# Expert rows carry their share and their token number, and are added into the tokens' rows in memory by scattering DMAs, instead of being gathered back at the end

## The chip, the cores and the metric

The kernel runs on one core of one Trainium2 chip. The metric is device microseconds of that core for one execution of the whole program. Before the change the median of three runs is 2100.1 us (2098.34 to 2104.96). Engines are called PE (matrix engine), DVE (vector), ACT (scalar), POOL (GpSimd) and SP (sync, which here only issues DMAs).

## The reference

Two layers over x of 8 x 512 tokens with 256 features. Layer 0 is a bidirectional state-space block plus a top-1 mixture of experts; it is not touched by the change. Layer 1, cut to what matters:

```python
xn = layernorm(x)
x  = x + L1_attn(xn) + L1_ffn(xn)

# L1_attn: 16 heads of 16; scores * decay(|i - j|), clipped, softmax, values, output projection
# L1_ffn, over all 4096 tokens, 8 "experts" of which the last does nothing, top 2, capacity 512:
weights = softmax(x_flat @ router_w + router_b)
topk    = the two largest weights of a token, the rest 0
noop_w  = topk[:, -1]                       # the expert that passes the token through
sorted_indices = argsort(-mask, axis=0)[:cap]        # first 512 tokens of each real expert
inputs  = x_flat[used_idx] * sorted_mask             # (512, 7, 256)
h       = relu(inputs @ experts_inter)               # 256 -> 1024
out     = (h @ experts_out) * in_w                   # 1024 -> 256, times the token's weight
combined = zeros.at[used_idx].add(out)
combined = combined + x_flat * (noop_w * noop_mask)
```

## The kernel before

The change lies in the layer 1 part, which the profile shows from about 1105 us to the end. That part is one attention loop with other work slipped in.

**The attention loop.** `steps` (end of `tile_kernel`) lists 128 steps: 8 batches, 4 groups of 4 heads, 4 tiles of 128 query rows. In step n the program writes, for that n: `scores` of n (four products s_ps at L1379, four clips on DVE at L1384, four decay-and-max operations on DVE at L1386, and the negated maximum ng at L1390, once a step), the exponentials of step n-1 on ACT (L1394), the transposes of step n-2 (PE p_ps L1401, ACT copies pT L1402), and every second step the products with the values (o_ps L1410). ng is thus a clock of the loop: one at each step. When the four tiles of a group are done, `divide` sends the sums through memory: ACT copies them to os (L1420), SP stores od (L1421), one step later SP loads oT and sm back (L1431, L1432), one more step later DVE inverts sm (L1437), SP stores rd and loads rb (L1438, L1440), and two steps later DVE multiplies oT (L1443). After a batch's last group `finish` makes the output projection (PE fin L1323, ACT fo L1325, DVE x_sb L1327).

**Order.** The order on each engine is written out by hand: the whole loop stands in a manual schedule, and each engine runs its instructions in the order in which the Python code made them. Between the parts of a step, `fill` draws a piece of other work (first `urgent`: projections of the next batch and `finish`; then `idle`: the experts), and `more` draws from `rows` (the generator `combine`) when there is nothing else. SP, too, is one queue in program order: a DMA that waits holds all later ones.

**The experts.** First `late` ends layer 0, then `route1` finds two slots for each token, and `send_rows` scatters each token's row of xn1 into xd1 by 64 indirect DMAs on POOL (L1296) and begins the token's result x_sb (L1303) from the token's row x1, loaded at L1311, plus its pass-through part. `experts` then runs each of the 7 experts in two halves of 256 rows: load rows (L1209), transpose, two matrix layers (L1236, L1249), copy the result to e_yo (ACT L1254) and store it in yd1 (SP L1256).

**The end.** When the experts are through, `combine` takes the 32 token tiles one after the other, one for each call of `more`. For each it copies two slot numbers (DVE at L1316, in `turn`), issues two gathers from yd1 (POOL yg L1344), and for the tile six places earlier adds the two gathered rows, weighted with wsel, into x_sb (DVE L1358). With each batch's fourth tile `send` stores the batch in four DMAs of 128 KB (SP L1335), if `finish` has had its turn; otherwise `finish` sends it.

```python
held.append((i, [e2.tile([P, DM], FP, name="yg1", tag="row1", bufs=14) for _ in range(2)]))
...
if len(held) > 6:
    add(*held.pop(0))
```

Both e_xd and e_yo are drawn from one tag of two buffers, e_rows. x1, xd1 and yd1 are tensors in memory.

Of the kernel before, what the change touches and what calls it, by code (L numbers as in the profile page):

```python
# [37 lines left out]
NSLOT1 = NE1 * CAP  # L38
HALF = CAP // 2


# [16 lines left out]
def tile_kernel(ctx: ExitStack, tc: tile.TileContext, t, out: bass.AP):  # L58
# [35 lines left out]
    G.iota(iota_t, pattern=[[P, NTILE]], base=0, channel_multiplier=0, allow_small_or_imprecise_dtypes=True)  # L94
    iota_b = ctile("iota_b", [P, NBLK])
    G.iota(iota_b, pattern=[[1, NBLK]], base=0, channel_multiplier=0, allow_small_or_imprecise_dtypes=True)
    zero = ctile("zero", [P, DM])
    G.memset(zero, 0.0)
# [3 lines left out]
    yd0 = dram.tile([NBLK * P, DM], FP, name="yd0", tag="yd0")  # L102
    xd1 = dram.tile([NSLOT1, DM], FP, name="xd1", tag="xd1")
    yd1 = dram.tile([NSLOT1 + 1, DM], FP, name="yd1", tag="yd1")

    x1 = dram.tile([NT, DM], FP, name="x1", tag="x1")
    xtd = dram.tile([B, P, KC, S], FP, name="xtd", tag="xtd")
# [10 lines left out]
    def clear(dst, rows, lo, hi):  # L118

        n = rows // P  # L120
        A.dma_start(
            out=dst[: n * P, :].rearrange("(p r) d -> p r d", p=P)[:, lo:hi, :], in_=bc(zero, 1, [P, hi - lo, DM])
        )
# [275 lines left out]
    def route0():  # L399
# [29 lines left out]

        B3 = [P, NBLK, NE - 1]  # L430
        past = big.tile(B3, FP, name="past", tag="past")
        V.tensor_tensor(past, bc(end[:, : NE - 1], 1, B3), bc(iota_b, 2, B3), ALU.is_le)
# [48 lines left out]
    steps()  # L481
    l1c = tl = w_r = rb = w_q = w_o = w_uk = w_uv = w_kv = band = slot1 = wsel = proj1 = vt0 = qk0 = r1b = noop = None
    tls = ExitStack()
# [3 lines left out]
    with ExitStack() as es:  # L487
# [169 lines left out]
        def second_weights():  # L657

            nonlocal l1c, tl, w_r, rb, w_q, w_o, w_uk, w_uv, w_kv, band, slot1, wsel, proj1, vt0, qk0
            es.close()  # L660
# [13 lines left out]
            slot1 = ctile("slot1", [P, NTILE, 2], I32, l1c)  # L674
            wsel = [l1c.tile([P, NTILE], FP, name=f"wsel{k}", tag=f"wsel{k}") for k in range(2)]
            proj1 = ctile("proj1", [P, NTILE, NE], pool=l1c)
# [358 lines left out]
        with tc.manual_schedule(engines=ENGINES):  # L1035
# [39 lines left out]
            for n in range(N):  # L1075
# [43 lines left out]
                if n % 8 == 3 and n // 8 < NE1:  # L1119
                    e = n // 8  # L1120
                    clear(xd1, NSLOT1, TPB * e, TPB * (e + 1))
                    if e == 0:
                        A.dma_start(out=yd1[NSLOT1 : NSLOT1 + 1, :], in_=zero[0:1, :])
            last = batch[B - 1]
# [19 lines left out]
    with tc.tile_pool(name="a1", bufs=1) as p1, tc.tile_pool(name="a2", bufs=2) as p2, tc.tile_pool(  # L1144
# [9 lines left out]
        def route1():  # L1154
# [30 lines left out]

            V.tensor_tensor(noop, pr[:, :, NE1], mask[:, :, NE1], ALU.mult)


# [28 lines left out]
        def experts():  # L1217
            w1, xd = expert_w1(0), expert_rows(0, 0)
            yield
            for e in range(NE1):  # L1220
                w2 = e1.tile([P, FC, DM], FP, name="e_w2", tag="e_w2")
                Y.dma_start(out=w2, in_=t["eo"][e])
                for half in range(2):
                    at = slice(e * CAP + half * HALF, e * CAP + (half + 1) * HALF)
                    xdT = e1.tile([P, KC, HALF], FP, name="e_xdT", tag="e_xdT")
                    tp = bank("e_tp", [P, KC, HALF])
                    for k in range(KC):
                        for c in range(2):
                            T.transpose(tp[:, k, c * P : (c + 1) * P], xd[:, c, k * P : (k + 1) * P], ident)
                    A.copy(xdT, tp)  # L1230
                    yield
                    hT = e1.tile([P, FC, HALF], FP, name="e_hT", tag="e_hT")
# [10 lines left out]
                    elif e + 1 < NE1:  # L1243
                        w1, xd = expert_w1(e + 1), expert_rows(e + 1, 0)
                    yo = e2.tile([P, 2, DM], FP, name="e_yo", tag="e_rows")
# [87 lines left out]
        def send(b):  # L1333
            for i in range(b * TPB, (b + 1) * TPB):
                Y.dma_start(out=out[i * P : (i + 1) * P, :], in_=x_sb[:, i, :])  # L1335

        def combine():

            held = []
            for i in range(NTILE):  # L1340
                held.append((i, [e2.tile([P, DM], FP, name="yg1", tag="row1", bufs=14) for _ in range(2)]))
                at = turn(e2, i)
                for k in range(2):
                    G.indirect_dma_start(  # L1344
                        out=held[-1][1][k], out_offset=None, in_=yd1,
                        in_offset=bass.IndirectOffsetOnAxis(ap=at[:, k : k + 1], axis=0),
                        bounds_check=NSLOT1, oob_is_err=False,
                    )
                yield
                if len(held) > 6:  # L1350
                    add(*held.pop(0))
            for one in held:
                add(*one)

        def add(i, yg):
            xi = x_sb[:, i, :]
            for k in range(2):
                V.scalar_tensor_tensor(xi, yg[k], wsel[k][:, i : i + 1], xi, ALU.mult, ALU.add)  # L1358
# [290 lines left out]
```

## Time and profile before

| what | value |
|---|---|
| runs of the kernel | median 2100.1 us, 2098.34 to 2104.96, three runs |
| the profiled execution | 2129.08 us; span 2127.2 us; mean granted PE clock 0.929 |
| busy over the span | PE 88%, DVE 69%, ACT 55%, POOL 30% |
| layer 1 part | 1105 to 2127.2 us |
| scatters of `send_rows` | 64 on POOL, 1190.8 to 1318.2 us |
| experts | PE e_tp first at 1333.2, last e_yo at 1965.8 us |
| gathers of `combine` | 64 on POOL, 1969.6 to 2091.3 us |
| weighted additions of `combine` | 64 on DVE, 1994.6 to 2099.0 us, mean 479 ns |
| DMA, whole span | 263.67 MB; HBM read 193.44 MB, written 72.75 MB |

All times within the execution are microseconds from the start of the profiled span. "x4" is a number of instructions merged into a row, and the bracket at a row's end tells how long its engine was idle before and what ended that. A row of a stretch gives for each engine the busy time and the number of instructions that began in it, then the granted clock of PE (1.00 is full speed), the share of time that the 16 DMA engines were busy, and GB/s.

### The profile page before, as it was taken

The numbers are of one execution on the slowest core, as the hardware profiler recorded it, in microseconds if no ns is written. First come the engines' busy times: TensorE is split into PE (matmuls) and PEld (weight loads), VectorE is DVE, ScalarE is ACT, GpSimd is POOL, SyncE is SP. The second block draws the span as 40 slices with busy tenths as digits, with TensorE's granted clock in tenths as the row PEclk, the third lists the DMA queues.
The fourth block names the chain that finished last, engine by engine and source line by source line (L and its number), as shares of the span: only waits on it lengthen the run. The fifth ranks groups of instructions, "written<-read, shape, count | busy, mean of one in ns | idle before, by whom it ended". The sixth has DMA issues, their size and how long they took to land. (4 is left out here: it accounts for less than half of the span.)

```text
span 2127.2 us, 33330 instructions
## 1 busy us (share of the span) xinstructions
PE 1861.6 (88%) x11672; PEld 1231.4 (58%) x11672; DVE 1461.2 (69%) x3329; ACT 1179.0 (55%) x2545; POOL 643.6 (30%) x592
## 2 busy tenths in 40 slices
PE   5666999999999999986758788999999999999785
PEld 5333776767677677644535444656666666666443
DVE  5684757575575757687648886666666676767795
ACT  2243544445354544545327566777677777777663
POOL 0048645456464646345400353000000000000552
PEclk9877999999999999997858778999999999999787
DMA  7113745556555556435433342121221212221355
GB/s 259 58 55 128 239 154 190 182 170 208 169 199 181 179 172 193 126 110 158 142 96 110 104 136 76 65 96 61 66 80 62 97 59 87 65 74 56 95 108 95
DMA packets 156632, 263.67 MB, mean 124 GB/s; under 512 B 24906, under 2 KB 113022, under 8 KB 144562
## 3 DMA queue, kind: packets, MB, share of 16 engines
q1 hardware_dynamic: 124816, 144.70, 21.6%
q0 software_dynamic: 22320, 107.55, 16.4%
q10 hardware_dynamic: 9330, 9.31, 1.3%
q8 instruction: 92, 1.51, 0.3%
q14 instruction: 74, 0.61, 0.1%
HBM read 193.44 MB, written 72.75 MB: 125 GB/s over the span
## 5 line engine op out<-in xcount | busy, mean ns | idle before, releaser
L1384 DVE TENSOR_SCALAR s<-s_ps 128x512 f32<-128x512 f32 x512 | 317.8, 683 | 241.6 <-PE s_ps L1379 195.9
L1394 ACT ACTIVATE s<-s,ng 128x512 f32<-128x512 f32 x512 | 354.4, 727 | 32.8 <-DVE ng L1390 23.1
L1401 PE MATMUL p_ps<-ident,s 128*128 128x128 f32 x2048 | 301.5, 292 | 72.4 <-ACT pT L1402 61.6
L1401 PEld LDWEIGHTS p_ps<-ident,s 128*128 128x128 f32 x2048 | 247.6, 149 | 159.7 <-ACT pT L1402 91.4
L1402 ACT COPY pT<-p_ps 128x512 f32<-128x512 f32 x512 | 279.1, 590 | 91.0 <-PE p_ps L1401 63.3
L1386 DVE CUSTOM_DVE_ANT_0 s<-s,band 128x512 f32<-128x512 f32 x512 | 322.8, 688 | 0.0
L1344 POOL DMA_INDIRECT yg<-yd,at x64 | 68.3, 1067 | 705.1 <-ACT s L1394 650.4
L728 PE MATMUL pj<-xT,w_in 128*128 128x512 f32 x384 | 204.5, 660 | 16.0 <-DVE cv L741 14.2
L1379 PE MATMUL s_ps<-kT,qT 16*128 16x512 f32 x1024 | 174.1, 694 | 17.9 <-DVE s L1384 11.5
L541 PEld LDWEIGHTS h_ps<-xdT,w 128*128 128x128 f32 x1248 | 150.1, 193 | 21.0 <-issue 20.2
L541 PE MATMUL h_ps<-xdT,w 128*128 128x128 f32 x1248 | 153.7, 277 | 1.6 <-DMA w<-in_w_dram,w_idx 1.6
L741 DVE SCALAR_TENSOR_TENSOR cv<-pj,w_conv_w,cv 128x511 f32<-128x511 f32 (+2 forms) x192 | 143.1, 746 | 9.6 <-ACT cv L737 5.6
L559 PE MATMUL y_ps<-w,hT 128*128 128x256 f32 x624 | 147.4, 380 | 0.0
L904 POOL TENSOR_TENSOR au<-da,half 128x512 f32<-128x512 f32 x64 | 77.7, 1214 | 212.0 <-PE seg L920 108.1
L1410 PE MATMUL o_ps<-pT,vt 128*32 128x256 f32 x2048 | 139.0, 414 | 0.0
L559 PEld LDWEIGHTS y_ps<-w,hT 128*128 128x128 f32 x624 | 116.0, 191 | 32.1 <-issue 17.9
L728 PEld LDWEIGHTS pj<-xT,w_in 128*128 128x128 f32 x384 | 71.8, 205 | 100.3 <-issue 92.2
L978 POOL TENSOR_TENSOR yT<-yT,ex 128x512 f32<-128x512 f32 (+1 forms) x48 | 59.7, 1243 | 226.3 <-DVE ex L977 168.1
L1236 PE MATMUL e_hp<-e_xdT,e_w 128*128 128x256 f32 x448 | 121.7, 394 | 3.0 <-ACT e_xdT L1230 2.1
L1249 PE MATMUL e_yp<-e_w,e_hT 128*128 128x256 f32 x448 | 120.0, 390 | 0.2
L933 ACT ACTIVATE mt<-seg,mid 64x64 f32<-64x64 f32 x512 | 109.9, 310 | 0.8
L1410 PEld LDWEIGHTS o_ps<-pT,vt 128*32 128x32 f32 x2048 | 64.7, 117 | 77.5 <-issue 48.0
(275 smaller groups left out, 3028.8 us busy)
## 6 DMA issues: line engine op xcount, KB each, us to landing
ex<-exd SPq DMA_DIRECT2D x96, 128.0 KB
u<-in_u_dram SPq DMA_DIRECT2D x16, 512.0 KB
xtd<-xT SPq DMA_DIRECT2D x16, 512.0 KB
fr<-fdd SPq DMA_DIRECT2D x64, 128.0 KB
od<-os SPq DMA_DIRECT2D x32, 256.0 KB
xT<-xtd SPq DMA_DIRECT2D x15, 512.0 KB
e_w<-in_ei_dram SPq DMA_DIRECT2D x7, 1024.0 KB
e_w<-in_eo_dram SPq DMA_DIRECT2D x7, 1024.0 KB
```

Of the source, the lines that this page charges most:

```text
L541: T.matmul(hp[:, i, :], w1[:, k * FF + f * P : k * FF + (f + 1) * P], xdT[:, k * P : (k + 1) * P], start=(k == 0), stop=(k == KC - 1),)
L559: T.matmul(yp, hT[f // 4][:, f % 4, :], w2[:, f * DM : (f + 1) * DM], start=(f == 0), stop=(f == FC - 1))
L728: T.matmul(pj, w_in[:, k, o * P : (o + 1) * P], self.xT[:, k, :], start=(k == 0), stop=(k == KC - 1))
L741: V.scalar_tensor_tensor(cv[:, s:], pj[:, : S - s], conv_w[:, q, 3 - s : 4 - s], cv[:, s:], ALU.mult, ALU.add)
L1236: T.matmul(hp, w1[:, k, f * P : (f + 1) * P], xdT[:, k, :], start=(k == 0), stop=(k == KC - 1))
L1379: T.matmul(sp[i], self.q[r, cols], self.k[r, :], start=True, stop=True)
L1384: V.tensor_scalar(self.p[i], sp[i], -CLAMP, CLAMP, ALU.max, ALU.min)
L1386: V.tensor_tensor_reduce(out=self.p[i], in0=self.p[i], in1=band[:, at : at + S], scale=1.0, scalar=-3.0e38, op0=ALU.mult, op1=ALU.max, acc ...
L1394: A.activation(self.p[i], self.p[i], AF.Exp, bias=self.ng[:, i : i + 1])
L1401: T.transpose(pp[:, k, :], self.p[i][:, k * P : (k + 1) * P], ident)
L1402: A.copy(pT[i][:, :, cc * P : (cc + 1) * P], pp)
L1410: T.matmul(op[32 * i : 32 * i + 32, half * 2 * P : (half + 1) * 2 * P], self.v[:, k, h * (AD + 1) : h * (AD + 1) + 32], pT[i][:, k, :], st ...
```

## The change

A row sent to an expert gets 16 more columns: the 8 routing shares of its token and the token's number less 4096 (repeated 8 times). The experts' result is multiplied by the share as it leaves PSUM and is added by an indirect DMA straight into the token's row of x1 in memory; a row of an expert that holds no token (number 0, as cleared) goes to one of 128 spare rows at the end of x1. x_sb now holds only the pass-through part and the attention, and x1 is added to it at the end by eight loads of 512 KB that add (`accum_op`). Gone are yd1, its stores, the 64 gathers, the 64 weighted additions, wsel, and the loads of x1 into x_sb. e_yo has a tag of its own. A batch is stored with one DMA of 512 KB. The constant iota_b is made later, iota_n is new.

```diff
+DW = DM + 2 * NE
...
-    zero = ctile("zero", [P, DM])
+    zero = ctile("zero", [P, DW])
...
-    xd1 = dram.tile([NSLOT1, DM], FP, name="xd1", tag="xd1")
-    yd1 = dram.tile([NSLOT1 + 1, DM], FP, name="yd1", tag="yd1")
-    x1 = dram.tile([NT, DM], FP, name="x1", tag="x1")
+    xd1 = dram.tile([NSLOT1, DW], FP, name="xd1", tag="xd1")
+    x1 = dram.tile([NT + P, DM], FP, name="x1", tag="x1")
...
-            wsel = [l1c.tile([P, NTILE], FP, name=f"wsel{k}", tag=f"wsel{k}") for k in range(2)]
+            iota_n = ctile("iota_n", [P, NTILE], pool=l1c)
+            G.iota(iota_n, pattern=[[P, NTILE]], base=-NT, channel_multiplier=1, allow_small_or_imprecise_dtypes=True)
...
-                        A.dma_start(out=yd1[NSLOT1 : NSLOT1 + 1, :], in_=zero[0:1, :])
+                        A.dma_start(out=x1[NT:, :], in_=zero[:, :DM])
...
+            to_send["shares"] = pr
...
-                V.tensor_copy(wsel[k], slots_of(big, oh, pr, "w"))
...
         def expert_rows(e, half):
-            xd = e2.tile([P, 2, DM], FP, name="e_xd", tag="e_rows")
+            xd = e2.tile([P, 2, DW], FP, name="e_xd", tag="e_rows")
...
                     A.copy(xdT, tp)
+                    share = e2.tile([P, 2], FP, name="e_sh", tag="e_sh")
+                    V.tensor_copy(share, xd[:, :, DM + e])
+                    number = xd[:, :, DM + NE]
+                    none = e2.tile([P, 2], FP, name="e_no", tag="e_no")
+                    V.tensor_scalar(none, number, 0.0, pidx, ALU.is_equal, ALU.mult)
+                    V.scalar_tensor_tensor(none, number, float(NT), none, ALU.add, ALU.add)
+                    to = e2.tile([P, 2], I32, name="e_to", tag="e_to")
+                    V.tensor_copy(to, none)
...
-                        A.copy(yo[:, c, :], yp)
+                        A.mul(yo[:, c, :], yp, share[:, c : c + 1])
+                        G.indirect_dma_start(
+                            out=x1, out_offset=bass.IndirectOffsetOnAxis(ap=to[:, c : c + 1], axis=0),
+                            in_=yo[:, c, :], in_offset=None, bounds_check=NT + P - 1, oob_is_err=True,
+                            compute_op=ALU.add,
+                        )
                         yield
-                    Y.dma_start(out=yd1[at, :].rearrange("(c p) d -> p c d", p=P), in_=yo)
...
         def send_rows():
+                if c == 0:
+                    V.tensor_copy(to_send[b][:, :, DM : DM + NE], to_send["shares"][:, i : i + TPB, :])
+                    V.tensor_copy(to_send[b][:, :, DM + NE :], bc(iota_n[:, i : i + TPB], 2, [P, TPB, NE]))
...
-                V.scalar_tensor_tensor(x_sb[:, i, :], x, noop[:, i : i + 1], x_sb[:, i, :], ALU.mult, ALU.add)
+                V.tensor_scalar(x_sb[:, i, :], x[:, :DM], noop[:, i : i + 1], None, ALU.mult)
...
         def ask_rows(b):
-            to_send[b] = r1b.tile([P, TPB, DM], FP, name="xs", tag="xs", bufs=B)
-            Y.dma_start(out=to_send[b], in_=rows_of(xn1, b))
-            Y.dma_start(out=x_sb[:, b * TPB : (b + 1) * TPB, :], in_=rows_of(x1, b))
+            to_send[b] = r1b.tile([P, TPB, DW], FP, name="xs", tag="xs", bufs=B)
+            Y.dma_start(out=to_send[b][:, :, :DM], in_=rows_of(xn1, b))
...
         def send(b):
-            for i in range(b * TPB, (b + 1) * TPB):
-                Y.dma_start(out=out[i * P : (i + 1) * P, :], in_=x_sb[:, i, :])
+            Y.dma_start(out=rows_of(out, b), in_=x_sb[:, b * TPB : (b + 1) * TPB, :])
...
         def combine():
-            held = []
-            for i in range(NTILE):
-                held.append((i, [e2.tile([P, DM], FP, name="yg1", tag="row1", bufs=14) for _ in range(2)]))
-                at = turn(e2, i)
-                for k in range(2):
-                    G.indirect_dma_start(
-                        out=held[-1][1][k], out_offset=None, in_=yd1,
-                        in_offset=bass.IndirectOffsetOnAxis(ap=at[:, k : k + 1], axis=0),
-                        bounds_check=NSLOT1, oob_is_err=False,
-                    )
-                yield
-                if len(held) > 6:
-                    add(*held.pop(0))
-            for one in held:
-                add(*one)
-        def add(i, yg):
-            xi = x_sb[:, i, :]
-            for k in range(2):
-                V.scalar_tensor_tensor(xi, yg[k], wsel[k][:, i : i + 1], xi, ALU.mult, ALU.add)
-            b = i // TPB
-            if i % TPB == TPB - 1:
+            for b in range(B):
+                G.dma_start(out=x_sb[:, b * TPB : (b + 1) * TPB, :], in_=rows_of(x1, b), accum_op=ALU.add)
                 combined.add(b)
                 if b in finished:
                     send(b)
+                yield
```

In the order of the changed program the eight adding loads stand one behind the other on POOL. Only the first of them waits, for the last scattering addition. On SP the stores of batches 0 to 5 stand, each behind a wait for its adding load, between the od store of the loop's 27th group (batch 6, third group) and that of the 28th (batch 6, last group). `finish` of batch 6 adds into x_sb after step 119's ng, behind a wait for the seventh adding load; `finish` of batch 7 comes after the loop. The order on PE and on ACT is the same as before, apart from the ACT operation that takes the place of the copy at L1254.

More of the change, by code (lines that the diff above doesn't have):

```diff
@@ L94, in tile_kernel @@
     G.iota(iota_t, pattern=[[P, NTILE]], base=0, channel_multiplier=0, allow_small_or_imprecise_dtypes=True)
-    iota_b = ctile("iota_b", [P, NBLK])
-    G.iota(iota_b, pattern=[[1, NBLK]], base=0, channel_multiplier=0, allow_small_or_imprecise_dtypes=True)
-    zero = ctile("zero", [P, DM])
+    zero = ctile("zero", [P, DW])
     G.memset(zero, 0.0)
@@ L121, in clear @@
         A.dma_start(
-            out=dst[: n * P, :].rearrange("(p r) d -> p r d", p=P)[:, lo:hi, :], in_=bc(zero, 1, [P, hi - lo, DM])
+            out=dst[: n * P, :].rearrange("(p r) d -> p r d", p=P)[:, lo:hi, :],
+            in_=bc(zero[:, : dst.shape[1]], 1, [P, hi - lo, dst.shape[1]]),
         )
@@ L430, in route0 @@
         B3 = [P, NBLK, NE - 1]
+        iota_b = big.tile([P, NBLK], FP, name="iota_b", tag="iota_b")
+        G.iota(iota_b, pattern=[[1, NBLK]], base=0, channel_multiplier=0, allow_small_or_imprecise_dtypes=True)
         past = big.tile(B3, FP, name="past", tag="past")
@@ L481, in tile_kernel @@
     steps()
-    l1c = tl = w_r = rb = w_q = w_o = w_uk = w_uv = w_kv = band = slot1 = wsel = proj1 = vt0 = qk0 = r1b = noop = None
+    l1c = tl = w_r = rb = w_q = w_o = w_uk = w_uv = w_kv = band = slot1 = iota_n = proj1 = vt0 = qk0 = r1b = noop = None
     tls = ExitStack()
@@ L657, in second_weights @@
         def second_weights():
-            nonlocal l1c, tl, w_r, rb, w_q, w_o, w_uk, w_uv, w_kv, band, slot1, wsel, proj1, vt0, qk0
+            nonlocal l1c, tl, w_r, rb, w_q, w_o, w_uk, w_uv, w_kv, band, slot1, iota_n, proj1, vt0, qk0
             es.close()
@@ L1223, in experts @@
                 for half in range(2):
-                    at = slice(e * CAP + half * HALF, e * CAP + (half + 1) * HALF)
                     xdT = e1.tile([P, KC, HALF], FP, name="e_xdT", tag="e_xdT")
@@ L1244, in experts @@
                         w1, xd = expert_w1(e + 1), expert_rows(e + 1, 0)
-                    yo = e2.tile([P, 2, DM], FP, name="e_yo", tag="e_rows")
+                    yo = e2.tile([P, 2, DM], FP, name="e_yo", tag="e_yo")
                     for c in range(2):
```

## The prediction

> **What bounds the kernel now.** I read the page first (shares, slices, chain), then the start times of ng, one a step, then stretches between those times, then DVE's instructions in one step. The page's slices show that the attention part has three regimes: PE at 9 tenths while experts are slipped in, and at the end a stretch in which PE falls to 7 and 8 while POOL comes back.
>
> ```profile
> PE   5666999999999999986758788999999999999785
> DVE  5684757575575757687648886666666676767795
> POOL 0048645456464646345400353000000000000552
> PEclk9877999999999999997858778999999999999787
> ```
>
> The ng times are 1960.52, 1966.84, 1974.26 and 1979.44 for steps 109 to 112, then 1994.49 for step 113 and 2092.92 for the last, 127. So 14 steps take 98.43 us, 7.03 each, and one step takes 15.05. Cut at these times (columns: PE, weight loads, DVE, ACT, POOL, clock, DMA share, GB/s):
>
> ```profile
> 1884.06:1960.52 76.46, 72.98 (x529) 46.52 (x528) 53.56 (x137) 56.05 (x108) 0.00 (x0) 1.00 0.16 50
> 1960.52:1979.44 18.92, 14.47 (x137) 8.49 (x136) 16.18 (x45) 12.01 (x22) 7.72 (x8) 0.97 0.23 71
> 1979.44:1994.49 15.05, 9.30 (x56) 5.51 (x60) 5.23 (x15) 8.08 (x14) 4.96 (x5) 0.58 0.18 52
> 1994.49:2092.92 98.43, 80.66 (x598) 46.45 (x587) 96.90 (x266) 67.23 (x120) 55.61 (x52) 0.88 0.60 122
> 2092.92:2127.20 34.28, 13.42 (x76) 7.66 (x74) 9.08 (x21) 8.61 (x17) 0.00 (x0) 0.72 0.30 62
> ```
>
> While experts run, PE is busy 72.98 of 76.46 us: PE is the bound. From 1994.49 to 2092.92 DVE is busy 96.90 of 98.43 us: DVE is the bound there, and the last 34 us are a chain of single transfers and small operations. DVE's part of one such step:
>
> ```profile
> 2007.67 1.00 DVE L1358 SCALAR_TENSOR_TENSOR x_sb<-yg,wsel,x_sb 128x256 f32<-128x256 f32 x2
> 2008.59 0.16 DVE L1316 COPY at<-slot 128x2 int32<-128x2 int32 x1
> 2008.66 1.00 DVE L1358 SCALAR_TENSOR_TENSOR x_sb<-yg,wsel,x_sb 128x256 f32<-128x256 f32 x2
> 2009.57 0.16 DVE L1316 COPY at<-slot 128x2 int32<-128x2 int32 x1
> 2009.64 2.48 DVE L1384 TENSOR_SCALAR s<-s_ps 128x512 f32<-128x512 f32 x4
> ```
>
> Of the step's 7 us, 1.97 (2007.67 to 2009.64) is `combine`; clips, maxima and ng are the other 5.
>
> **The change, part by part.** The sum is made against the profiled execution (2129.08 us, span 2127.2); it is 29 us above the median 2100.1, and I carry the difference over unscaled.
>
> *The last 14 steps.* 50 of the 64 additions at L1358 start in them. Four cost 1.97 us with their two copies, so 12.5 times 1.97 is 24.6 us of DVE that go; 98.43 less 24.6 is 73.8, 5.3 a step. Single steps without slipped-in work took 5.0 to 5.2 (step 28: 1328.54 to 1333.59; step 112: 1974.26 to 1979.44), but no two stand in a row. ACT is next: 67.23 us busy, 91% of 73.8. So I take 5.5 a step, 77.0: a gain of **21.4**, between 24.6 and 11.
>
> *The 15 us step.* DVE was done at 1979.6; ACT stood 8.43 us before a copy:
>
> ```profile
> 1984.24 0.59 ACT L1402 COPY pT<-p_ps 128x512 f32<-128x512 f32 x1 [8.43 <-remote]
> ```
>
> The trace doesn't name what ended it. All ten pauses of this kind in the trace, 28.6 us together, lie while POOL issues indirect DMAs (1204 to 1303 and 1984 to 1986), none in the experts' stretch. If they follow the number of POOL's DMAs (128, so 0.22 us each), the 36 new ones bring 8 of the 9.3 back; if they need several in quick succession, only the eight loads can bring one. The gain lies between 1 and 10; I take **5**. Copies of `at` in the two steps before: **0.3**.
>
> *Scattering additions.* 28 on POOL, about 1.0 us each by the rows of the scatters and gathers, on an engine that stood idle for 650 us. Each waits for the one before; the two of a half are 9.2 us apart (e_yo at 1956.57 and 1965.80). Nothing but the next one is queued behind, and e_yo has two buffers a tile, so a landing of up to 9 us costs nothing, and a longer one only after a half has been overtaken. Taken as 0, the last one excepted, which the adding loads wait for. The stores of yd1 leave SP, where 89.1 us of waits for e_yo stood ahead of od stores; since sm and rb were rarely late, worth 0.
>
> *Small operations with the experts.* 56 on DVE at about 0.17 us (row of ng and `at`): 9.5 us over 14 places. PE's work covers them; without that cover they cost 9.5. I take **+1**. ACT's product instead of a copy: 393 ns (L1239, same shape) against 373, 28 times, 0.6 us, covered.
>
> *Sending.* 32 operations of 477 ns (L1303) become one-input ones, between 286 ns (L1190) and 409 ns (L628): 2.2 to 6.1 us less. Sixteen copies of 0.18 add 2.9; two products, two sums and two copies of wsel (0.42, 0.42, 0.18) take 2.0 away. DVE is busy 103 of 134 us there; about half counts: **-2**. Wider rows (1088 B for 1024), the 4 MB of x1 loads that go and the later iota_b (DVE needs it at 148.1, POOL is idle from 141.5) change nothing that is waited for.
>
> *The eight adding loads.* No row shows one. Copying through POOL's queue took 27.4% of 18 us for 1.44 MB (1968 to 1986), and 44.1% of 92 us for 6.00 MB later: 1.7 to 3.5 us for 512 KB. The Trainium skill, page "Collectives: The Full Stack", section "The bandwidth ceiling: the fold count and why AG ≠ RS ≠ AR", speaks against them: an adding transfer reads two sources where a copy reads one, and runs at about half the rate. By the rows alone the loads take 1.7 to 3.5 us each, by the rule 3.4 to 7. POOL's issue may bind instead: 128 rows take 1.31 us from gather to gather, and a load has 512, so 1.3 to 5.2. I take 4. If the last scattering addition lands at about 1972, the sixth load is there at 1996 (1982 to 2014).
>
> That load counts because of SP. The od store of batch 6's last group, wanted two us after step 113's ng (before: 1996.53 after 1994.49; then: 1986), stands behind six output stores that wait for six loads. From od to sm took 6.8 us at the end (2102.53 to 2109.3), and DVE's inversion of sm stands after step 116's ng, at about 2001. sm is then there at 2003 (1989 to 2021): a stop of DVE, and of the loop behind it, of 2 to 3 us (0 to 20). **+3**. The addition of `finish` for batch 6 waits for the seventh load only at step 119, 16 us later.
>
> A second rule bears on the issue: "SBUF — State Buffer", section "SBUF: two separate sides", says that DVE and GpSimd hold a shared port pair in turn, each for a whole operation, that GpSimd cannot write descriptors while DVE works in a two-port mode, and that DVE operations with two SBUF inputs shut out GpSimd operations that read SBUF. If the maxima (two inputs, 4 x 0.61 of 5.3 us) count against the loads' descriptors, 8 x 4 us of issue stretch to about 60. The row of this trace says no: gathers kept 1.01 us (median) in a stretch with DVE busy 98%. I follow the row; the rule is the slow rival's reason.
>
> *The end.* Its chain of od, sm, rd, rb and fin stays. The last store is 512 KB behind the last addition instead of 128 KB: by od (256 KB in 2.01 us) about **+1.1**.
>
> Sum: -21.4 - 5 - 0.3 - 2 + 1 + 3 + 1.1 = -23.6. Span 2104, median 2100.1 - 23.6 = **2076.5**.
>
> **The rivals.**
> *Another engine takes the step.* For: ACT at 91%, and PE's clock was 0.88, with 3.57 us for a half-rate o_ps group against 1.86. Against: less DVE time packs PE more densely, which kept the clock at 1.00 with experts. With 6.2 us a step the gain in the loop is 11.6: 2086.
> *SP's hold takes back most of it.* Loads at 7 us: sixth at 2014, sm at 2021, a stop of 20 instead of 3, and the ACT pause comes back (1 instead of 5): 2097. Against: nothing forces the upper end.
> *Slower: the adding loads crawl.* One mechanism: POOL's descriptors or the add itself, at the place where SP holds od. Gain and loss meet when the stop is 26.6, sm at 2027.6, the sixth load at 2021: 8.1 us a load, 65 GB/s. At 10 us a load the sixth lands at 2032, the stop is 38: 2111. For: no adding DMA has a row. Against: copies in the same queue run at 150 to 300 GB/s.
>
> **How the numbers follow.** Likeliest case as worked (2064 to 2086): 0.66. Another engine, 2082 to 2092: 0.14. SP's hold, 2090 to 2106: 0.11. Crawling loads, above 2106: 0.09. A measurement here can tell 0.3%, 6.3 us, from no change: faster means below 2093.8, slower above 2106.4. Faster: 0.66, 0.14 and 0.02 of the third, 0.82; within: 0.09; slower: 0.09. Range: 2064 to 2098, leaving out the crawling loads, half of the hold and a little below.
>
> **What would show it.** Right: ng from step 113 to 127 in 74 to 80 us with DVE busy over 90%; no step of 15 us; adding loads 3 to 5 us apart in landing; PE over 94% busy with experts as before. Wrong: DVE idle before the inversion of sm or the addition of `finish` after step 119, waiting for a DMA (loads); DVE at 80% with ACT or PE packed (another engine); experts' steps longer than 8.5 and 6.3 us in turn (small operations or pauses of ACT at each scattering addition).

## The result and the profile after

The changed kernel took 2088.23 us (median of five, 2081.71 to 2089.04) against 2100.1 us before (2096.8 to 2104.96, five runs on the same chip). The ratio is 0.9928 [0.9911, 0.9944]: 11.9 us faster, half of the 23.6 forecast. The profiled execution of the changed kernel took 2089.04 us, with a span of 2087.3 us.

The slices of PE and POOL from its page, to be laid beside those of before:

```profile
PE   5666999999999999978776888999999999999875
POOL 0048645446464544545420065000100000010200
```

The block of POOL at the end (552 before, the gathers) has shrunk to one slice of 2, the adding loads. PE's row hardly differs: a slice is 52 us wide, and what changed has to be cut out at the ng times. The stretches answer to those shown before: experts, the end of the experts, step 113, the last 14 steps, the rest (columns as there):

```profile
1862.83:1939.22 76.39, 73.26 (x524) 47.52 (x520) 53.92 (x140) 55.16 (x107) 4.64 (x3) 0.98 0.19 51
1939.22:1958.04 18.82, 17.09 (x158) 10.05 (x157) 15.84 (x41) 15.36 (x28) 10.18 (x9) 1.00 0.50 82
1958.04:1963.09 5.05, 3.69 (x39) 2.16 (x41) 5.01 (x14) 4.59 (x9) 1.88 (x2) 1.00 1.21 202
1963.09:2052.40 89.31, 68.87 (x589) 40.31 (x580) 73.76 (x190) 66.44 (x120) 0.00 (x0) 0.90 0.36 90
2052.40:2087.30 34.90, 14.38 (x82) 8.38 (x80) 2.92 (x7) 8.61 (x17) 0.00 (x0) 0.76 0.12 39
```

Step 113 takes 5.05 us instead of 15.05. The last 14 steps take 89.31 us instead of 98.43, and DVE is busy in only 73.76 of them: 23.1 us of DVE's work left this stretch, 9.1 us of time did. The difference lies in one step. Up to its start and after its end the steps are short:

```profile
1958.04:1978.22 20.18, 16.78 (x163) 10.01 (x162) 20.04 (x52) 18.67 (x34) 1.88 (x2) 1.00 1.18 229
1978.22:1995.69 17.47, 5.96 (x26) 3.40 (x28) 5.30 (x14) 4.50 (x9) 0.00 (x0) 0.70 0.50 139
1995.69:2052.40 56.71, 49.83 (x440) 29.07 (x432) 53.43 (x137) 47.86 (x87) 0.00 (x0) 0.94 0.10 35
```

The first row is four steps of 5.05 us with DVE busy 20.04 of 20.18: that is DVE's floor, lower than the 5.5 of the forecast. The second row is step 117 alone: 17.47 us in which no engine is busy for more than 6. DVE in it:

```profile
1990.53 0.35 DVE L1435 RECIPROCAL sm<-sm 128x32 f32<-128x32 f32 x1 [12.14 <-DMA sm<-od]
```

DVE waited 12.14 us for sm, so it wanted it at 1978.4. The DMA queue of SP says why sm was late:

```profile
1955.99 19.87 SPq L1352 DMA_DIRECT2D out_dram<-x_sb  x6
1975.95 0.54 SPq L1419 DMA_DIRECT2D od<-os  x1
...
1986.39 0.51 SPq L1429 DMA_DIRECT2D oT<-od  x1
1986.94 0.51 SPq L1430 DMA_DIRECT2D sm<-od  x1
```

The six output stores, each behind its adding load, hold SP from 1956 to 1975.9. Then od is issued. The load of oT that reads it back (1986.39) waits until it has landed, 10.4 us later; the load of sm follows, and DVE has sm at 1990.5: 14.6 us from od to the inversion.

### The profile page after: what moved, and what is told of

It is laid out like the page before. It is cut to its first block, busy times and chain, and to the rows that moved or that the text cites. A ratio compares the mean times of both kernels' runs of the same rounds, so it can differ in the third digit from the quotient of the medians.

```text
span 2087.3 us, 33144 instructions
## 1 busy us (share of the span) xinstructions
PE 1838.5 (88%) x11672; PEld 1219.8 (58%) x11672; DVE 1434.2 (69%) x3299; ACT 1176.7 (56%) x2545; POOL 624.6 (30%) x565
## 5 line engine op out<-in xcount | busy, mean ns | idle before, releaser
L1399 PE MATMUL p_ps<-ident,s 128*128 128x128 f32 x2048 | 286.1, 283 | 48.8 <-ACT pT L1400 48.8
L1399 PEld LDWEIGHTS p_ps<-ident,s 128*128 128x128 f32 x2048 | 236.5, 144 | 128.3 <-ACT pT L1400 86.0
L1267 POOL DMA_INDIRECT x<-e_yo,e_to x28 | 44.6, 1592 | 601.1 <-ACT e_yo L1266 540.5
L1377 PE MATMUL s_ps<-kT,qT 16*128 16x512 f32 x1024 | 164.0, 671 | 27.5 <-DVE s L1382 21.0
L544 PEld LDWEIGHTS h_ps<-xdT,w 128*128 128x128 f32 x1248 | 150.1, 194 | 21.4 <-issue 20.8
L745 DVE SCALAR_TENSOR_TENSOR cv<-pj,w_conv_w,cv 128x511 f32<-128x511 f32 (+2 forms) x192 | 143.1, 746 | 10.9 <-ACT cv L741 6.9
L1261 PE MATMUL e_yp<-e_w,e_hT 128*128 128x256 f32 x448 | 120.1, 391 | 0.2
```

The lines of the kernel that those rows point to most:

```text
L544: T.matmul(hp[:, i, :], w1[:, k * FF + f * P : k * FF + (f + 1) * P], xdT[:, k * P : (k + 1) * P], start=(k == 0), stop=(k == KC - 1),)
L1261: T.matmul(yp, hT[:, f, c * P : (c + 1) * P], w2[:, f, :], start=(f == 0), stop=(f == FC - 1))
L1377: T.matmul(sp[i], self.q[r, cols], self.k[r, :], start=True, stop=True)
L1399: T.transpose(pp[:, k, :], self.p[i][:, k * P : (k + 1) * P], ident)
```

## Where the time before had been taken: two kinds of chips

The profiled execution of before was 29.0 us above the median of its own runs. Later runs show that the chip that a run gets makes a difference of this size. The kernel before took 2100.1, 2102.7 and 2099.9 us (medians) on three occasions, and 2127.7 and 2129.2 on two others. Profiles from the second kind show the pauses of ACT that the trace calls "remote", those of the first kind show none. They lie beside bursts of indirect DMAs and nowhere else: in `send_rows`, and in the steps where `combine` gathers. The `send_rows` stretch (steps 9 to 27) takes 117 to 120 us without them and 138 to 153 with them. The experts' stretch takes 651 to 655 us on both kinds, at a granted clock of 0.99 to 1.00, so the two kinds differ in some stages and not in all.

The pauses mark the slower stages, but their sum does not account for them: in the changed kernel of `after_again` they are 12.9 us, and its `send_rows` stretch is 34 us longer than in the first profile after (150.7 against 116.6). No chip with a number on record was used twice, so "kind of chip" may be a kind of the chip or its state at the time. The profile that stands before the prediction is of the second kind; the runs beside it and the first profile after are of the first. Every ratio below is to the kernel before on the same chip.

The kernel before without pauses (`before_third`, `send_rows` stretch and last 14 steps):

```profile
1187.72:1307.82 120.10, 102.10 (x768) 57.66 (x764) 113.67 (x322) 89.93 (x162) 66.58 (x64) 0.88 0.41 135
1967.40:2065.89 98.49, 83.05 (x594) 48.48 (x583) 96.96 (x266) 67.22 (x120) 56.49 (x53) 0.84 0.61 124
```

Its step 113 takes 5.2 us, not 15, and its 14 steps 98.5, as in the profile shown first: the long step belonged to the pauses, the slow 14 steps did not.

## The experiments

**before_again and after_again: both kernels as they are, for further profiles.**

> The kernel before once more, for a second profile of it. If the ten pauses of ACT (28.6 us, all beside POOL's indirect DMAs) belong to the kernel, they come back and the span is near 2127 us. If they belonged to that one execution, the span is near 2100 us, step 113 takes about 5.2 us instead of 15.0, and steps 9 to 27 about 129 us instead of 148.6. I lean to the second, 0.75, since the median of the runs is 29 us under the profiled execution.

> The changed kernel once more, on the same chip as the others of this call. Ratio to the kernel before 0.993. In the profile the stop of DVE before the inversion of sm after step 116 (12.1 us) comes back, since it follows from the order on SP; the start of the loop (ng of step 0), 6.5 us later than in the kernel before, comes back if wider clears or constants cause it, and not if it is scatter of one execution.

Measured on a chip with pauses: before 2127.72 us (2123.18 to 2131.62), the profiled execution 2133.98; after 2113.9 (2111.53 to 2115.84), ratio 0.9936 [0.9914, 0.9958]. The pauses of before came back, 17.6 us in all, so the leaning to a single odd execution (0.75) was wrong; after has 12.9 us of them too, all in `send_rows`. Step 113 takes 12.7 us before and 5.0 after. The later start of the loop did not come back (1106.9 after, 1112.9 before). The stop of step 117 did, in the same place:

```profile
2015.66 0.35 DVE L1435 RECIPROCAL sm<-sm 128x32 f32<-128x32 f32 x1 [11.75 <-DMA sm<-od]
```

What follows: the gain is 12 to 14 us on either kind of chip, and the stop belongs to the changed kernel.

**after_late: the six output stores put off, one a step from step 117 on.**

```diff
 def send(b):
-    Y.dma_start(out=rows_of(out, b), in_=x_sb[:, b * TPB : (b + 1) * TPB, :])
+    if n < 117: waiting.append(b)
+    else: store(b)
...
+                if n >= 117 and waiting:
+                    store(waiting.pop(0))
```

> The changed kernel, but the output stores of batches 0 to 5 are put off to steps 117 to 122, one a step, so that the od store of batch 6's last group neither waits on SP behind them nor stands in their queue. If the stop of 12.1 us comes from those stores, it goes wholly: 14 steps in about 77 us instead of 89, time 11 to 13 us under the changed kernel, ratio to before about 0.987. If it comes from the adding loads themselves taking the DMA engines, od and sm still share the engines with them and half of the stop or more stays: ratio 0.990 or above.

Measured: 2100.68 us (2097.86 to 2107.37), ratio 0.9871 [0.9849, 0.9893], 13.2 us below the changed kernel on the same chip. Its last 14 steps, and the inversion of sm that had waited:

```profile
1994.50:2070.31 75.81, 65.38 (x582) 38.26 (x574) 73.67 (x191) 66.72 (x120) 0.00 (x0) 0.95 0.42 107
```

```profile
2009.91 0.35 DVE L1443 RECIPROCAL sm<-sm 128x32 f32<-128x32 f32 x1
```

Nothing else was changed, the stop is gone (no bracket), and the time fell by about its length. This kernel beats both.

**before_nocomb: the kernel before without gathers and weighted additions.**

```diff
-    held.append(...); at = turn(e2, i); G.indirect_dma_start(...) x2
-    if len(held) > 6: add(*held.pop(0))
```

> The kernel before without the gathers and the weighted additions of combine (the experts' results never reach the output); everything else, and the stores of the output, stay. It gives the ceiling of what freeing DVE in the last steps can bring. If DVE's work there is the bound in undisturbed executions too, the 14 steps from 113 to 127 take 74 to 77 us instead of 98.4, and the time falls by 22 to 26 us, ratio about 0.989. If ACT or PE takes over at 6 us or more a step, it falls by less than 14 us.

Measured: 2096.42 us (2093.45 to 2101.43), ratio 0.9858 [0.9832, 0.9884], 31.3 us below before on that chip, more than the 22 to 26 expected, since step 113 takes 5.0 us here too and had taken 12.7. The 14 steps:

```profile
1984.99:2061.24 76.25, 66.00 (x592) 38.60 (x580) 73.51 (x190) 66.51 (x120) 0.00 (x0) 0.96 0.22 71
```

So after_late reaches, within the error, what taking the whole of `combine` away gives. The scattering additions and adding loads cost nothing that shows in their own stretches: the experts' take 652.4 us in after_late and 652.7 here, the 14 steps 75.8 and 76.2. The 4.3 us between the two times, whose intervals overlap, are not there: the stretch from the first ng to step 27 is 10.7 us longer in after_late.

**after_tiny and after_poolstore: which part of the store makes sm late.** In the first the six stores stay in SP's order with their waits, but carry 1 KB each. In the second POOL issues them, in full, behind its eight loads.

```diff
 # after_tiny, for b < 6
+    Y.dma_start(out=out[b * S : b * S + 1, :], in_=x_sb[0:1, b * TPB, :])
 # after_poolstore, in combine behind the loop of the loads
+    for b in sorted(finished - sent):
+        send(b, G)
```

> The changed kernel with the six early output stores left where they stand on SP, each still behind the wait for its adding load, but each only one row of 1 KB: most of the output of batches 0 to 5 is left out. In the changed kernel DVE wanted sm at 1978.4 us and stood 12.1 us. If it is bytes (the od store queued behind 3 MB of output stores, engines full), what is left is at most SP's hold: od issued when the sixth load has landed, sm 6.8 us later, so a stop of 0 to 4.5 us, step 117 in 5 to 10 us, and a time 8 to 13 us below the changed kernel, about 0.988 to 0.990 of the kernel before. If it is SP's wait for the loads, step 117 keeps some 17 us and the time stays at 0.993 to 0.994.

> The changed kernel with the six early output stores issued by POOL, behind its eight adding loads: the same 3 MB at about the same time, but not on SP, so neither SP's hold nor a place in SP's queue ahead of od. If the stop comes from the place in SP's queue (hold or bytes ahead), step 117 takes 5 to 6.5 us and the time is that of the kernel with the stores put off, 0.987 of the kernel before. If it comes from the share of the DMA engines that loads and stores take, whoever issues them, od and sm still land late: a stop of 6 us or more, and 0.990 to 0.994.

Measured: after_tiny 2108.1 us (2100.54 to 2113.74), 0.9893 [0.9864, 0.9921]; after_poolstore 2108.31 (2105.18 to 2125.11), 0.9912 [0.9881, 0.9943]. Both lie between the changed kernel and after_late, with intervals that overlap theirs; the traces tell them apart (one of each). In each kernel DVE wants sm 15.3 us after step 113's ng (after: 1978.4 less 1963.09). Counted from that ng:

| kernel | od issued | from its issue to its landing | from there to the inversion of sm | DVE's wait |
|---|---|---|---|---|
| after | 12.9 | 10.4 | 4.2 | 12.1 |
| after_tiny (SP held, no bytes) | 8.2 | 5.5 | 3.9 | 2.35 |
| after_poolstore (bytes, SP not held) | 2.0 | 8.4 | 10.9 | 6.0 |
| after_late (neither) | 2.0 | 8.2 | at most 5.1 | 0 |

A landing is read from the load of oT that waits for it. The rows behind it, after_tiny first, then after_poolstore:

```profile
2004.28 0.35 SPq L1422 DMA_DIRECT2D od<-os  x1
...
2009.81 0.51 SPq L1432 DMA_DIRECT2D oT<-od  x1
2013.71 0.35 DVE L1438 RECIPROCAL sm<-sm 128x32 f32<-128x32 f32 x1 [2.35 <-DMA sm<-od]
```

```profile
2003.45 0.51 SPq L1434 DMA_DIRECT2D sm<-od  x1
2013.75 0.35 DVE L1439 RECIPROCAL sm<-sm 128x32 f32<-128x32 f32 x1 [6.00 <-DMA sm<-od]
```

after_tiny came out as the first of its two alternatives, bytes. SP's hold alone costs 2.35 us. The bytes add 9.8 us to it in the changed kernel, in about equal parts. SP is held 4.7 us longer, since the adding loads that it waits for land 4.4 us apart beside the stores and 2.65 us apart without them; and od takes 4.9 us more to land behind 3 MB of stores.

after_poolstore came out as its second alternative by its numbers, but od did not land late: 8.4 us, against 8.2 without any stores. POOL's stores stand behind its loads and moved mainly after od had landed: from 2003 to 2013.7 POOL's queue moved 3.35 MB, and what was late beside them is the 8 KB of sm. So stores issued elsewhere cost a wait too, but a different one, and its 6.0 us are no part of the 12.1. Whether the 4.9 us of od come from its place behind the stores in SP's own queue, or from their share of the DMA engines, these runs don't divide.

**after_late4: besides, the last batch stored in four DMAs.**

```diff
+                if b == B - 1:
+                    Y.dma_start(out=out[i * P : (i + 1) * P, :], in_=x_sb[:, i, :])
```

> The changed kernel with the six stores put off, one a step from step 117 on, and besides the last batch stored in four DMAs of 128 KB, each behind its own addition, instead of one of 512 KB behind the fourth. By the term of the forecast for the end (1.1 us) the time is about 1 us below the kernel with the stores put off: ratio 0.986 to 0.987, and the stretch from the last ng to the end 34.3 us instead of 35.4. If the end is bound by the chain of od, sm, rd and rb alone, nothing changes: 35.4.

Measured: 2101.19 us (2098.81 to 2110.97), ratio 0.987 [0.9844, 0.9896]; from the last ng to the end 36.2 us, against 35.4 in after_late (on another chip). No gain.

**before_gathers and before_adds: one half of `combine` at a time.**

```diff
 # before_gathers: no V.scalar_tensor_tensor at L1358
 # before_adds: no turn, no gathers
+    held.append((i, [zero, zero]))
```

> The kernel before with its 64 gathers but without the 64 weighted additions: the experts' results never reach the output. Theory: the long step 113 comes with the burst of gathers on POOL (a pause of ACT), the slow 14 steps with DVE's additions. Then step 113 stays at 12 to 15 us, the 14 steps take about 76, and the time is some 20 us below the kernel before, ratio about 0.990. Rival: both come with the additions, or the pause has nothing to do with gathers: step 113 takes 5 us and the time is that of the kernel without gathers and additions, ratio 0.986, 10 us lower.

> The kernel before with its 64 weighted additions, but without the 64 gathers and the copies of slot numbers: the additions read a tile of zeros that lies in SBUF, so the experts' results never reach the output. It is the counterpart of the kernel with gathers and no additions, which gained nothing (97.4 us for the last 14 steps, 12.5 for step 113). Theory now: two limits of about the same height stood one behind the other in the last 14 steps, DVE's additions and the pauses and clock dips that come with the gathers. Then step 113 takes 5 us (it has no additions yet), the 14 steps keep 93 to 97 us with DVE busy (96.9 less 3.2 of slot copies), and the time is 10 to 14 us below the kernel before, ratio 0.993 to 0.995. Rival: the gathers alone were the limit, and DVE's busy share was filling: 14 steps in 76 to 82, ratio 0.986 to 0.989.

before_gathers ran on a chip with pauses: 2131.39 us (2119.47 to 2139.09), ratio 1.0004 [0.9989, 1.0019]. Step 113 stayed at 12.5 us, as the theory had it: the long step comes with the gathers. But its main number and the rival's were both wrong. Without a single weighted addition the 14 steps still take 97.4 us:

```profile
1988.19:2085.61 97.42, 75.11 (x586) 42.48 (x590) 76.99 (x216) 68.63 (x122) 53.58 (x52) 0.87 0.59 121
```

DVE is busy only 76.99 us of it, and no other engine over 75.11. The time is in ACT's waits for copies of pT, and perhaps in PE's clock (0.87 against 0.96 in before_nocomb). ACT in step 113 and in one of the 14 steps, from the same trace:

```profile
1977.46 0.58 ACT L1399 COPY pT<-p_ps 128x512 f32<-128x512 f32 x1 [5.45 <-remote]
...
2009.27 1.07 ACT L1399 COPY pT<-p_ps 128x512 f32<-128x512 f32 x2 [4.24 <-PE p_ps L1398]
```

before_adds ran on a chip without pauses: 2099.8 us (2094.25 to 2107.56), ratio 0.9993 [0.9982, 1.0005]. The 14 steps take 97.2 us with DVE at its limit, as expected:

```profile
1967.10:2064.30 97.20, 80.60 (x590) 46.96 (x580) 95.15 (x241) 67.00 (x120) 0.00 (x0) 0.84 0.18 57
```

The 10 us expected of step 113 did not come, since on this chip there was no pause to take away. The gain of 10 to 14 us that had been expected was 2.9 us by the medians, within the noise. DVE's additions alone hold the loop at 97 us.

**before_third and gathers_again: the two open sides of this.**

> The kernel before once more, for its profile. Its time has come out at 2100 to 2103 us on two chips and at 2128 to 2129 us on two others. Theory: the 27 us between them are the pauses of ACT beside indirect DMAs, which some chips show and others not. On a chip near 2100: no pause in the profile, a send stage of 117 to 122 us, step 113 in 5 to 7 us, and the 14 steps in 97 to 100. On a chip near 2128: a send stage of 139 to 149, step 113 in 12 to 15, 14 steps in 98 to 101. Rival: the chips differ in something that touches all stages, and the experts' 85 steps differ too from 651 to 655.

> The kernel before with the gathers and without the weighted additions (the experts' results never reach the output), once more. It gained nothing (1.0004) on a chip where the kernel before takes 2129 us. Theory: there the pauses that come with the gathers held the 14 steps at 97 us. On a chip near 2100, without pauses, the 14 steps then take 76 to 80 us and the ratio is 0.988 to 0.991; on a chip near 2128 it is 1.000 again. Rival: the gathers hold the loop without any pauses, through POOL or the DMA engines: 14 steps in 90 or more and a ratio of 0.997 to 1.000 on either chip.

Measured on a chip without pauses: before 2099.91 us (2092.45 to 2104.65). before_third, whose profile is the one shown above, came out as its theory had it: no pause, 120.1 us for `send_rows`, 5.2 for step 113, 98.5 for the 14 steps, and 654.3 for the experts, which the rival had expected to differ.

gathers_again took 2096.44 us (2086.68 to 2102.4), ratio 0.9979 [0.9967, 0.9991], the 14 steps in 92.4 us. The rival won, in its numbers (0.9979 and over 90 us) and, in one step, in its mechanism: the gathers hold back the gain without any pauses. They don't slow the loop as a whole. Of steps 114 to 126 most take 5.2 to 5.6 us, little more than in after_late. But step 127 takes 18.4 us. DVE wants rb there at 2040.5, and SP at that time:

```profile
2052.87 0.69 DVE L1440 TENSOR_TENSOR oT<-oT,rb 128x512 f32<-128x512 f32 x1 [12.39 <-DMA out_dram<-x_sb]
```

```profile
2029.94 0.33 SPq L1435 DMA_DIRECT2D rd<-sm  x1
2038.97 0.59 SPq L1437 DMA_DIRECT2D rb<-rd  x1
2039.61 9.10 SPq L1335 DMA_DIRECT2D out_dram<-x_sb  x4
```

The bracket names an output store, but the chain was late before any of them was issued. The load of rb waits until rd, a small store, has landed: 9.0 us here, against 1.4 to 3.7 for every other such pair within the last 14 steps in all the profiles. And once rb was issued, its 256 KB hardly moved for 9 us. The DMA queues from 2039 to 2048 (q0 is POOL's, here the gathers; q1 is SP's; the last figure is the share of the 16 DMA engines' time):

```profile
q0 software_dynamic: 255, 0.69, 98.3%
q1 hardware_dynamic: 3, 0.01, 0.2%
```

The gathers take nearly all of the DMA engines' time, and only 77 GB/s move in all. From 2048 to 2053, with their share at 23.3%, SP's queue moved 1.14 MB, rb and output stores, and DVE went on. So it is not the stop of the changed kernel, which large stores made: here, as far as one trace can tell, the gathers themselves held rd and rb back. Without the stop the 14 steps are 80.0 us (92.4 less 12.4); on the chip with pauses no stop of this kind is in the trace, and they took 97.4. So one gain was lost in two ways: to pauses, and perhaps the clock, on the one kind of chip, to a wait of 12.4 us on the other.

**after_spread: after_late with 56 gathers more, in the experts' stretch, that nobody reads.**

```diff
+    for k in range(2):
+        spare = e2.tile([P, DW], FP, name="spare", tag="spare", bufs=4)
+        G.indirect_dma_start(out=spare, in_=xd1, in_offset=...at[:, k : k + 1]...)
```

> The changed kernel with the six stores put off, and with 56 gathers of 128 rows added that nobody reads, two behind each of the 28 scattering additions, so that POOL issues three indirect DMAs in some 4 us and then nothing for about 5 to 7 us, all through the experts' stretch. If ACT's pauses go by the number of indirect DMAs (0.22 us each), ACT shows some 12 us of pauses in the experts' stretch and this grows from 652 us by up to 12, PE being the limit there. If they need a burst, as of 64 behind one another, it stays at 651 to 655 and no pause over 2 us appears between steps 27 and 112; the time is that of the kernel with the stores put off, 0.987.

Measured on a chip without pauses: 2074.82 us (2070.55 to 2079.22), ratio 0.9881 [0.9855, 0.9906]. The experts' 85 steps take 651.4 us, what they take without the extra gathers. As there was no pause on this chip even in `send_rows`, the run doesn't decide what it was made for. The five profiles of changed kernels on chips with pauses tell more, for the additions: each has pauses in `send_rows`, where 64 indirect DMAs stand some 2 us apart, and none in the experts' stretch with its 28, where 0.22 us each would have made 6.2. So the number of indirect DMAs alone is not the rule. That it takes a burst is the likeliest reading, but the two stretches differ in other things too.

## Why the prediction was right, and where its sizes were off

The direction and the main mechanism held: DVE's additions bounded the 14 steps, the loop then ran at DVE's new floor, and the price was paid in a wait for sm behind SP's stores, at the place that was named. The number, 2088.23, is less of a success than its place in the range says. It lies above the likeliest case (2064 to 2086), among the numbers of "another engine" (2082 to 2092), which did not happen; what happened besides the gain is the rival of SP's hold (2090 to 2106), with a stop of over half its 20 us. That the range reached up to 2098 for this rival is what makes the forecast hold. Of the signs named beforehand, step 113, the adding loads (3.1 to 4.4 us apart) and PE beside the experts (73.26 of 76.39 us) came as signs of being right. But the 14 steps took 89.31 us with DVE busy 83%, instead of 74 to 80 and over 90%, and DVE idle before the inversion of sm, waiting for a DMA, stood in the list as a sign of being wrong.

The terms, with before_third and the first profile after (both without pauses, on different chips):

| term | forecast | measured |
|---|---|---|
| last 14 steps, the stop taken out | -21.4 | -21.3 (98.49 to 77.17) |
| the 15 us step, copies of `at` | -5.3 | -0.2 (5.2 to 5.0) |
| sending (first ng to step 27) | -2 | -0.3 (195.2 to 194.9) |
| small operations, experts | +1 | -3.1 (654.3 to 651.2) |
| SP's hold and adding loads | +3 | +12.1 |
| the end | +1.1 | -0.5 (35.4 to 34.9) |
| up to the first ng | 0 | -0.8 |
| sum | -23.6 | -14.1 (spans 2101.3 to 2087.3; medians -11.9) |

*The last 14 steps.* Right to 0.1 us, by luck in part: the quiet steps took 5.0 rather than 5.5, others had work slipped in and took up to 6.7. ACT and PE did not take over.

*The 15 us step.* The second largest error. The step was real in the profiled execution, but not in the runs that gave the 2100.1 us: "it is 29 us above the median 2100.1, and I carry the difference over unscaled". The stages with pauses made that difference: beside before_third, the stretch from the first ng to step 27 was 28.0 us longer in it and step 113 9.8 us, and the rest 12 us shorter. A gain from one of these stages could not show in a median without them. On chips with pauses step 113 does fall, from 12.7 to 5.0, more than the 5 us taken. Of that little shows in the whole (13.8 us gained there, 11.9 here), since the `send_rows` stretch was longer after: 146.4 to 152.5 us in all five changed kernels on such chips, 138.5 to 148.6 in the four kernels with the old `send_rows`. The forecast's gain of 2 us in sending is thus a loss of some 7 on these chips. What brings it, the wider rows or something else, was not tested.

*SP's hold.* The term that failed most: 12.1 us instead of 3. DVE wanted sm at 15.3 us after step 113's ng (forecast 17: 2001 less 1984), which was near enough. od was issued at 12.9 (forecast 12: 1996 less 1984), which was right by luck: loads at 2.65 us each, as in after_tiny, release it at 8.2, and the output stores between the loads, which the forecast gave no time, made up the rest. The third part was "From od to sm took 6.8 us at the end": a duration from a stretch in which the DMA engines moved 62 GB/s was put into one in which they moved 245 (1976 to 1986.4). There it took 14.6. 12.9 + 14.6 - 15.3 is the 12.2 us stop. It lies inside the bounds given for the term (0 to 20), and the rival that prices it, SP's hold, had the right place and a wrong cause: not slower loads, but the stores between and ahead.

*The adding loads.* By the moved bytes:

```profile
q0 software_dynamic: 1673, 1.67, 109.4%
```

This is 1951 to 1961, before the first store had a share: 1.67 MB of adding loads in 10 us, 3.1 us for 512 KB, their start included. From 1961 to 1976, with the output stores beside them, 1.84 MB in 15 us, 4.3 us each. The forecast's 4 holds for the mixture. The Trainium skill's rule ("Collectives: The Full Stack", section "The bandwidth ceiling: the fold count and why AG ≠ RS ≠ AR") is stated there for the adding step (ReduceScatter) of a collective among several ranks; carried over to these loads it put 3.4 us at the lower end. Alone the loads stayed below it (2.65 us apart in after_tiny), inside the rows' own 1.7 to 3.5. Crawling loads (8.1 us) were never near. The second rule of the forecast, "SBUF — State Buffer", section "SBUF: two separate sides", had made some 60 us of an issue of 8 x 4 us, if DVE's maxima count against it. The same reckoning with the forecast's lower figure, 1.3 us a load, would be an estimate of 19 us. POOL issued all eight in 10.39 us, with DVE busy 10.32 of them. So the maxima did not hold these loads up, and not following the rule was right; whether any operation of DVE here works in the two-port mode of which the page speaks, no row shows:

```profile
1945.34 1.66 POOL L1267 DMA_INDIRECT x<-e_yo,e_to  x1 [7.78 <-ACT e_yo L1266]
1949.52 10.39 POOL L1357 DMA_DIRECT2D x_sb<-x  x8 [2.52 <-DMA x<-e_yo,e_to]
```

The first of them waits 2.52 us for the last scattering addition, and no other instruction waits for one. An addition occupies POOL for 1.59 us in the mean, where 1.0 was taken, and nothing waits for that either. ACT's product took 474 ns instead of 393, covered by PE's work.

*Sending, small operations, the end.* Experts' stretches of both kernels scatter from 651 to 655 us, so -3.1 shows only that the 56 small operations cost nothing that can be seen. Sending took DVE from 113.67 to 109.40 us in its main stretch (steps 9 to 27), which fell by 3.5 us (120.1 to 116.6); but steps 0 to 9 took 3.2 us more (75.1 to 78.3), and why is open. The last store costs nothing, whole or in four.

*What the forecast did not see.* That DVE was not the only limit of the 14 steps. Leaving out the additions alone gives 0.998 to 1.000, leaving out the gathers alone 0.999, both together 0.986 (on a chip with pauses; on one without, after_spread, which has neither in these steps, gives 0.988). The change pays because it removes both, and the argument from DVE's 98% alone would have given the same 21 us to a kernel that kept the gathers.

*What stays open.* What ends the "remote" pauses of ACT, and why some chips show them; how the 97.4 us of before_gathers divide between the pauses and PE's lower clock, and whether the clock is a cause there or follows from the waits. Whether 56 extra gathers in the experts' stretch would bring pauses on a chip that has them was not measured.

## What to carry to other kernels

A busy share of 98% says that an engine is a limit, not that it is the only one: before counting on the gain, ask what the loop does when only that engine's work is gone. A transfer's duration is taken from a stretch with the same traffic, and a store that nobody waits for is put behind the small transfers that a loop waits for: the stores here were worth 13 us by their place alone. A wait's label names what came last, and not always what was late: follow the chain back to its first transfer. Where a profiled execution is far above the median of the runs, first find the difference in the trace, and count no gain from it.

## What had not been expected of the hardware

Scattering with addition, 128 rows of 1 KB onto rows in memory, held POOL 1.59 us (a gather 1.03 in the same stretch of after_spread), and 28 of them, some 23 us apart in the mean, left a loop that PE bounds at its 651 us. In one stretch of gathers_again the gathers took 98% of the DMA engines' time while moving only 77 GB/s, and a small store beside them landed after 9.0 us instead of 1.4: the GB/s of a stretch don't say how full the engines are. Bursts of indirect DMAs came with pauses of ACT of up to 11 us on some chips and with none on others. The kernel before takes 27 us more on the chips with pauses, and the longer stages are those in which they lie; eight plain adding loads of 512 KB in a burst brought none on either.
